# Attention and experts in one kernel: layer norm spread over two rounds a batch, routing one piece a round, tokens' transposes in other banks and ahead of the scores, idle matmuls at the start

## The chip, the cores and the metric

The kernel runs on one core of a Trainium2 chip. The core has a matrix engine (TensorE, PE in the profile), a vector engine (VectorE, DVE), a scalar engine (ScalarE, ACT), GpSimd (POOL) and SyncE (SP), which here only issues transfers. Each works through its own list of instructions in order and waits on semaphores for the others. The metric is the time of one execution on the device, in microseconds (us); less is better.

## The reference, cut to what matters

The input x has 8 batches of 512 tokens of 256 numbers, all in float32. Attention has 16 heads of 64, and the expert part has 16 experts with 1024 hidden units and 256 places each.

```python
xn  = layernorm(x)                                   # over the 256, eps 1e-5
# attention
q, k, v = split(xn @ qkv_w.T)                        # 16 heads of 64
q, k = rope(q), rope(k)
kb  = -max(p, .01) * log1p(max(a, .01) * |i - j|)    # a and p per head
attn = softmax(q @ k.T / 8 + kb)
att = concat(attn @ v) @ out_w.T
# experts
gate = softmax(xn @ Wg); idx = argmax(gate)          # one expert a token
loc  = place of the token among those of its expert  # kept if loc < 256
ffn  = relu(dispatched @ w1) @ w2, gathered back, times its gate
out = x + att + ffn
```

## The kernel before

**Steps and rounds.** The 16 heads are taken in 4 groups of 4. A step s is one group and one batch (32 steps, s = 8 g + b), and a step has four rounds (128 in all; d counts them, `dd` is d modulo 4). Each round projects one of q and k of a head pair for the next step (`project_qk`), computes the scores of the next round's two query chunks (`score`), and turns the exponentials of this round's two (`turn`, DVE transposes in blocks of 32). `project_v` makes the values in the first two rounds of a step. At the end of odd rounds `move` sends a pair's turned exponentials across partitions with 16 transfers of 128 KB and three small ones, all issued by SP. Four rounds later `attend` multiplies them with the values and `attended` scales the result on DVE; `project_out` adds a finished step's output to y, in the first round of a step two steps later.

**Order.** The order of the instructions on every engine is the order in which the program writes them (the schedule is manual). What the main loop (L819) says in round d therefore stands on each engine's list behind all that earlier rounds put there. Lists `later` and `stores` hold transfers until a later round; `stores` is emptied on POOL, one a round in rounds 0 and 1, and up to three a round after that.

**Layer norm.** In the first group each batch passes: load (`load_x`, L88), `moments` on DVE (L187: four pairs of statistics and aggregation), `deviations` (L193: three small operations on DVE, and a Newton iteration of 15 small ones on POOL, or of 10 on DVE), `normalise` on ACT (L231: four operations of 256 columns), `transpose_normed` (L246: eight PE transposes into two banks, and two copies of 512 columns), `logits` and `turn_logits` (L265, L278). The normalised tokens (to xrd) and their transposes (to xnd) are stored by POOL. The three later groups, and steps from 3 on in the first, read the transposes back (`load_normed`, on SP).

**Banks.** The accumulator's eight banks are four pools: `ps_sc` 4 (scores), `ps_mm` 2 (projections, values, output sums, expert hidden units), `ps_av` 1 (attention), `ps_po` 1 (logits, routing, expert output). A matmul into a bank waits until the bank's last reader is done.

**Start.** L785 to L815 are the work ahead of round 0: the rotation's tables, the bias tables of two head pairs (Ln on ACT), batch 0 and batch 1 normalised and transposed, q and k of both pairs of step 0. Round 0's loop body comes after two units of scores.

**Routing and experts.** `route` (L291) is a generator: each `yield` ends a piece. The loop takes two pieces a round from round 11 (L889), until all 18 are done. Two rounds after that, in round 22, `expert_in(0)` runs, and from round 23 `expert_work` (L522) gives units: four of hidden and four of output for each of 16 experts, 128 in all. A round takes 0, 1, 3 (4 in every fourth step) and 2 units, by its place in the step (L905). Weights of the next expert are loaded by SP into the same two buffers when the units that read them are done. The units must be over before round 108 (`late`), since results are gathered from there.

Of the kernel before, what the change touches and what calls it, by code (L numbers as in the profile page):

```python
# [9 lines left out]
F32 = mybir.dt.float32  # L10
I32 = mybir.dt.int32
BF16 = mybir.dt.bfloat16
AF = mybir.ActivationFunctionType
# [4 lines left out]
B, S, DM, H, D = 8, 512, 256, 16, 64  # L18
E, F = 16, 1024
P = 128  # L20
NTOK = B * S
NT = NTOK // P
TB = S // P
# [3 lines left out]
GC = HG * D  # L27
# [6 lines left out]
def attention_and_experts(  # L34
# [13 lines left out]
    nc = tc.nc  # L48
# [34 lines left out]
    wg = const.tile([P, 2, 32], F32, name="wg")  # L83

    first = zpool.tile([P, TB, TB, DM], F32, tag="z", name="xin_first")
    xin: dict = {b: first[:, b] for b in range(TB)}

    def load_x(b, eng):  # L88
        if b >= TB:
            xin[b] = early.tile([P, TB, DM], F32, tag="xin", name=f"xin_{b}", bufs=XB)  # L90
        eng.dma_start(xin[b], x[b].rearrange("(n p) d -> p n d", p=P))

    def load_group(g, eng):
        wq = wpool.tile([P, 2, 3 * GC], F32, tag="wq", name=f"wq_{g}")
# [6 lines left out]

    nc.scalar.dma_start(fr, freqs)
    nc.scalar.dma_start(ab[:, 0, :], bias_a.partition_broadcast(P))
    load_x(0, nc.sync)
    nc.gpsimd.dma_start(ab[:, 1, :], bias_p.partition_broadcast(P))
    weights = {0: load_group(0, nc.scalar)}
    nc.vector.memset(wg, 0.0)
# [12 lines left out]
    def bias_tables(g, pair, stage):  # L120

        for j in range(2):
            h = g * HG + 2 * pair + j
            if stage == 0:
                kb[h] = kbpool.tile([P, TB, KBW // P, 32], F32, tag="kb", name=f"kb_{h}")
                nc.scalar.activation(
                    kb[h], dist, AF.Ln, bias=1.0, scale=ab[:, 0, h : h + 1]
                )
            if stage == 1:
# [54 lines left out]
    rstd = const.tile([P, NT], F32, name="rstd")  # L184
    off = const.tile([P, NT], F32, name="off")

    def moments(b):  # L187
        for n in range(b * TB, (b + 1) * TB):
            st = early.tile([P, 6], F32, tag="st", name=f"bn_{n}", bufs=3)
            nc.vector.bn_stats(st, xin[b][:, n % TB, :])  # L190
            nc.vector.bn_aggr(mv[:, n, :], st)
# [51 lines left out]
        )  # L243
        xns[b] = xn

    def transpose_normed(b, pool=ps_mm, tag="mm", copy=nc.scalar.copy):  # L246
        xn = xns.pop(b)
        if b < 3:
            xnT = xpool.tile([P, 2, S], F32, tag="xnT", name=f"xnT_{b}")
            xnTs[b] = xnT  # L250
        else:
            xnT = early.tile([P, 2, S], F32, tag="xt", name=f"xnT_{b}", bufs=2)
        for mc in range(2):
            pt = pool.tile([P, S], F32, tag=tag, name=f"xt_{b}_{mc}")
            for i in range(TB):
                nc.tensor.transpose(
                    pt[:, i * P : (i + 1) * P], xn[:, i, mc * P : (mc + 1) * P], ident
                )
            copy(xnT[:, mc, :], pt)  # L259
        stores.append(lambda: nc.gpsimd.dma_start(xnd[b], xnT))  # L260
        xns[b] = xnT

    lgT: dict = {}

# [26 lines left out]
    def route():  # L291
# [131 lines left out]
        for part in range(4):  # L423
            for n in range(8 * part, 8 * part + 8):
                nc.vector.tensor_scalar(
                    rows[part][:, n % 8, :], slot, loc[:, n : n + 1], None, ALU.is_equal
                )
# [138 lines left out]
    def project_v(s, i2):  # L566
        g, b = divmod(s, B)
        wq, _ = weights[g]
        if i2 == 0:
            vals[s] = qkpool.tile([P, TB, GC], F32, tag="v", name=f"v_{s}")  # L570
        ps = ps_mm.tile([P, 2, GC], F32, tag="mm", name=f"v_{s}_{i2}")
        for i in range(2):
            c0 = (2 * i2 + i) * P
            for mc in range(2):
                nc.tensor.matmul(  # L575
                    ps[:, i, :], xnTs[s][:, mc, c0 : c0 + P], wq[:, mc, 2 * GC :],
                    start=(mc == 0), stop=(mc == 1),
                )
        nc.scalar.copy(vals[s][:, 2 * i2 : 2 * i2 + 2, :], ps)
# [198 lines left out]
    steps = NG * B  # L778
# [35 lines left out]
    k1 = project_qk(0, 1, 1, False)  # L814
    turn_by(nc.vector, k1[2], k1[0], k1[1], slice(0, S))  # L815

    routing = route()
    working = begin = None
    for d in range(duos):  # L819
# [39 lines left out]
        if d in (1, 3) or 5 <= d <= 10:  # L859
            turn_logits(d - 3 if d > 3 else d // 2)  # L860
        if dd in (0, 1):
            project_v(s, dd)
        (turn_last if final else turn)(*units[2 * d + 1])
        if dd == 1 and 3 <= s + 2 < steps:
            load_normed(s + 2)
        if half and not final:
            move(s, pair)
# [2 lines left out]
            later.append(lambda s=s: store_y(s - 2, s - 2 >= steps - B + 2))  # L870


        if d in (0, 2) or 4 <= d <= 9:
            logits(d - 2 if d > 2 else d // 2)
        if d in (2, 4, 6, 7):
            normalise(d)
        if d in (2, 4):
            normalise(d + 1)
        if d < 4:
            moments(d + 2)  # L880
        if d in (5, 6):
            moments(d + 1)
        if d == 1:
            deviations(2, 4, nc.gpsimd)
        if d == 3:
            deviations(4, 6, nc.gpsimd)
        if d in (5, 6):
            deviations(d + 1, d + 2, nc.gpsimd)
# [116 lines left out]
```

## Time and profile before

| what | value |
|---|---|
| median of 3 runs | 1298.36 us (1293.68 to 1299.41) |
| the profiled execution | 1296.84 us, span 1295.1 us |
| busy in the span: PE, DVE, ACT, POOL | 1222.4, 898.8, 612.3, 607.7 us |
| TensorE clock granted, mean | 0.98 |
| first scores start (L598) | 28.1 us |
| transfers | 264.66 MB, 204 GB/s |

The profile is one execution taken by the hardware profiler. A line of the busy-time view gives a stretch and the busy us of each engine in it. A line of the view of waits says which instruction waited for which, the us in total, how often, and the longest. In a timeline a line gives start, duration, engine, source line, operation, the tile written and the tiles read, sizes and how many; in square brackets stands the idle time before it and what ended it. PEld is PE's loading of weights, SPq an instruction that issues a transfer. A matmul in float32 is two instructions in the trace. The engines' shares are averages over parts with different limits, so the first 240 us have to be read by themselves.

### The profile page before, as it was taken

What the parts mean: (1) busy time and instruction counts of PE and PEld (TensorE: products, weight loads), DVE (VectorE), ACT (ScalarE), POOL (GpSimd) and SP (SyncE); (2) the same over time, 40 slices, a digit from 0 to 9 for tenths busy, and PEclk for the clock granted to TensorE, in tenths of its full rate; (3) what the DMA queues carried; (4) which work ended last, traced back from release to release, by engine and by line L of the source; (5) the groups of instructions that cost most, each with busy time, mean ns of one, the idle gap of its engine ahead of it and who ended that gap; (6) DMA issues with size and microseconds to landing.
All of it is one profiled execution on the core that took longest, in us unless ns stands there. A gap on an engine that the chain in (4) does not pass through costs nothing.

```text
span 1295.1 us, 17166 instructions
## 1 busy us (share of the span) xinstructions
PE 1222.4 (94%) x4986; PEld 664.9 (51%) x4986; DVE 898.8 (69%) x2270; ACT 612.3 (47%) x1425; POOL 607.7 (47%) x569
## 2 busy tenths in 40 slices
PE   4877999999999999999999999999999999999877
PEld 1334434455555555555555555556555555444434
DVE  6967899866556666566666666666666666888762
ACT  5565434544544434444464434344346443466551
POOL 3666434633543444444444434353344433578840
PEclk9988999999999999999999999999999999999988
DMA  4388778788867788878777688698788676889995
GB/s 131 84 245 275 190 176 214 209 209 213 224 190 194 206 216 216 246 181 229 202 192 224 171 222 215 180 242 213 198 214 234 169 208 156 223 223 229 237 234 141
DMA packets 184797, 264.66 MB, mean 204 GB/s; under 512 B 32176, under 2 KB 96448, under 8 KB 184704
## 3 DMA queue, kind: packets, MB, share of 16 engines
q1 hardware_dynamic: 177232, 241.51, 72.2%
q0 software_dynamic: 6368, 20.99, 5.6%
q10 hardware_dynamic: 1104, 1.07, 0.2%
q8 instruction: 40, 0.66, 0.2%
q14 instruction: 53, 0.43, 0.1%
HBM read 99.91 MB, written 31.44 MB: 101 GB/s over the span
## 4 chain that ended last, share of the span: by engine, by line
PE 73%; DMA 8%; DVE 7%; SPq 5%; ACT 4%; issue 2%; POOL 1%; ACTq 0%; DVEq 0%; POOLq 0%
PE sc L598 14%; PE av L691 14%; PE qk L549 14%; PE ph L494 8%; PE po L509 8%; PE v L575 7%; PE po L730 7%; SPq L636 4%; DMA pt<-z 4%; DVE z L609 2%; DVE z L622 1%; ACT z L613 1%; DMA w<-in_w 1%; SPq L644 1%; DMA early<-yd 1%
## 5 line engine op out<-in xcount | busy, mean ns | idle before, releaser
L562 POOL TENSOR_TENSOR t<-t,cos_t 128x512 f32<-128x512 f32 (+1 forms) x126 | 160.9, 1277 | 592.6 <-ACT t L558 587.2
L613 ACT ACTIVATE z<-z,st 128x512 f32<-128x512 f32 x512 | 363.3, 711 | 51.2 <-DVE st L609 34.8
L609 DVE CUSTOM_DVE_ANT_1 z<-sc,kb 128x512 f32<-128x512 f32 x512 | 322.7, 686 | 30.1 <-PE sc L598 24.8
L622 DVE STREAM_TRANSPOSE z<-z 128x512 f32<-128x512 f32 x504 | 320.1, 682 | 0.0
L598 PE MATMUL sc<-t,t 64*128 64x512 f32 x1024 | 258.3, 621 | 5.9 <-DVE t L564 3.6
L549 PE MATMUL qk<-xnT,wq 128*128 128x512 f32 x512 | 251.3, 615 | 6.9 <-ACT xnT L259 3.0
L558 ACT COPY t<-qk 128x512 f32<-128x512 f32 x125 | 73.0, 584 | 376.5 <-DVE sh L553 374.2
L691 PE MATMUL av<-pt,v 128*64 128x512 f32 x1008 | 233.8, 606 | 4.5 <-DMA rb<-rd 3.3
L598 PEld LDWEIGHTS sc<-t,t 64*128 64x128 f32 x1024 | 90.2, 188 | 165.5 <-issue 143.8
L553 DVE LOAD_MASK_SELECT sh<-qk x128 | 1.8, 14 | 244.5 <-PE qk L549 241.0
L564 POOL TENSOR_TENSOR t<-t,sh 128x512 f32<-128x512 f32 (+1 forms) x126 | 160.7, 1275 | 9.9
L563 POOL TENSOR_TENSOR sh<-sh,sin_t 128x512 f32<-128x512 f32 (+1 forms) x126 | 161.1, 1279 | 0.0
L691 PEld LDWEIGHTS av<-pt,v 128*64 128x64 f32 x1008 | 68.3, 138 | 161.6 <-issue 146.9
L549 PEld LDWEIGHTS qk<-xnT,wq 128*128 128x128 f32 x512 | 97.0, 196 | 91.7 <-issue 70.5
L575 PE MATMUL v<-wq,xnT 128*128 128x256 f32 x512 | 127.1, 392 | 8.2 <-ACT t L558 5.8
L730 PE MATMUL po<-wo,o 128*128 128x256 f32 x512 | 125.3, 388 | 2.9 <-ACT xnT L259 2.3
L494 PE MATMUL ph<-xdT,w 128*128 128x256 f32 x512 | 120.0, 385 | 4.6 <-ACT hT L500 1.9
L509 PE MATMUL po<-w,hT 128*128 128x256 f32 x512 | 120.8, 384 | 1.9 <-ACT hT L500 1.0
L575 PEld LDWEIGHTS v<-wq,xnT 128*128 128x128 f32 x512 | 95.8, 193 | 45.9 <-DVE z L622 21.1
L730 PEld LDWEIGHTS po<-wo,o 128*128 128x128 f32 x512 | 95.1, 191 | 39.4 <-ACT t L558 12.1
L494 PEld LDWEIGHTS ph<-xdT,w 128*128 128x128 f32 x512 | 95.2, 190 | 34.0 <-ACT t L558 6.8
L509 PEld LDWEIGHTS po<-w,hT 128*128 128x128 f32 x512 | 94.7, 190 | 31.1 <-issue 12.7
(145 smaller groups left out, 799.8 us busy)
## 6 DMA issues: line engine op xcount, KB each, us to landing
pt<-z SPq DMA_DIRECT2D x1008, 128.0 KB
w<-in_w SPq DMA_DIRECT2D x64, 512.0 KB
rb<-rd SPq DMA_DIRECT2D x126, 128.0 KB
xnT<-xnd SPq DMA_DIRECT2D x29, 512.0 KB
yd<-y SPq DMA_DIRECT2D x26, 512.0 KB
y<-yd SPq DMA_DIRECT2D x24, 512.0 KB
xrd<-xn POOLq DMA_DIRECT2D x8, 512.0 KB
xnd<-xnT POOLq DMA_DIRECT2D x8, 512.0 KB, 4.9
```

Of the source, the lines that this page charges most:

```text
L494: nc.tensor.matmul(ph[:, i, :], held["w1", e, fc // 4][:, mc, (fc % 4) * P : (fc % 4 + 1) * P], xdT[:, mc, :], start=(mc == 0), stop=(mc = ...
L509: nc.tensor.matmul(po[:, c, :], hT[:, fc, c * P : (c + 1) * P], held["w2", e, fc // 4][:, fc % 4, :], start=(fc == 0), stop=(fc == F // P ...
L549: nc.tensor.matmul(ps, wq[:, mc, c0 : c0 + P], xnTs[s][:, mc, :], start=(mc == 0), stop=(mc == 1),)
L562: eng.tensor_tensor(t[:, c], ps[:, c], cos_t[:, c], ALU.mult)
L563: eng.tensor_tensor(sh[:, c], sh[:, c], sin_t[:, c], ALU.mult)
L575: nc.tensor.matmul(ps[:, i, :], xnTs[s][:, mc, c0 : c0 + P], wq[:, mc, 2 * GC :], start=(mc == 0), stop=(mc == 1),)
L598: nc.tensor.matmul(sc[j].rearrange("p (g c k) -> p g c k", g=TB, k=32), q[r, qc * P : (qc + 1) * P], k[r, :].rearrange("p (c g k) -> p g c ...
L609: nc.vector.tensor_tensor_reduce(z, sc[j].rearrange("p (g c k) -> p g c k", g=TB, k=32), bias, -0.125, 3.0e38, ALU.add, ALU.min, st[:, j : ...
L613: nc.scalar.activation(z, z, AF.Exp, bias=st[:, j : j + 1], scale=-1.0, accum_out=sums[s, pair][:, j, qc : qc + 1],)
L622: nc.vector.transpose(z, z)
L691: nc.tensor.matmul(av[j * D : (j + 1) * D, :].rearrange("p (a q) -> p a q", q=P), vals[s][:, kc, c0 : c0 + D], pts[s, pair][:, j, :, kc, : ...
L730: nc.tensor.matmul(ps[:, i, :], oTs[pair][:, c0 : c0 + P], wot[:, pair, :], start=(pair == 0), stop=(pair == 1),)
```

## The change

The loads of x change place: batch 0 comes in two halves, batch 3 takes a buffer of y. Ahead of round 0, 42 idle matmuls of the identity (20, 8 and 14) are put into PE's list, batch 1's moments are split around batch 0's copies, its deviations go to POOL, the DVE turns 256 instead of 128 columns of q, and batch 1's transposes move behind the first scores. In the loop a batch's moments are taken in halves in two rounds (`moments_at`), it is normalised in a round of its own (`normal_at`) and transposed in the next but one or the next (`turned_at`), ahead of that round's scores. The transposes go to the banks of attention and of logits (for batch 2, of attention and projections) instead of the projections' two; the first half of the values goes to the attention's bank. Routing starts at round 16 with one piece a round, and the 32 compares yield every four instead of every eight. The experts take 1, 1, 4 and 2 or 3 units a round. The new stage 2 of `bias_tables` is called nowhere.

```diff
-    xin: dict = {b: first[:, b] for b in range(TB)}
-    def load_x(b, eng):
-        if b >= TB:
+    xin: dict = {b: first[:, b] for b in range(3)}
+    def load_x(b, eng, parts=1):
+        if b == 3:
+            xin[b] = ypool.tile([P, TB, DM], F32, tag="y", name=f"xin_{b}")
+        if b > 3:
...
-    load_x(0, nc.sync)
+    load_x(0, nc.sync, 2)
...
-    def moments(b):
-        for n in range(b * TB, (b + 1) * TB):
+    def moments(b, halves=(0, 1)):
+        for n in [b * TB + 2 * h + i for h in halves for i in range(2)]:
...
-    def transpose_normed(b, pool=ps_mm, tag="mm", copy=nc.scalar.copy):
+    def transpose_normed(b, copies=None):
         xn = xns.pop(b)
-        if b < 3:
+        if b < 4:
...
         for mc in range(2):
+            pool, tag = ((ps_av, "av"), (ps_mm, "mm") if b == 2 else (ps_po, "po"))[mc]
...
+    def keep_warm(n):
+        idle = ps_sc.tile([P, P], F32, tag="sc", name=f"idle_{len(idles)}")
+        idles.append(idle)
+        for _ in range(n):
+            nc.tensor.matmul(idle, ident, ident, start=True, stop=True)
...
+                if n % 4 == 3:
+                    yield
             if part > 1:
                 gathered(0, part - 2)
-            yield
...
-        ps = ps_mm.tile([P, 2, GC], F32, tag="mm", name=f"v_{s}_{i2}")
+        pool, tag = ((ps_av, "av"), (ps_mm, "mm"))[i2]
+        ps = pool.tile([P, 2, GC], F32, tag=tag, name=f"v_{s}_{i2}")
...
     bias_tables(0, 1, 0)
+    keep_warm(20)
     moments(0)
     deviations(0, 1, nc.vector)
     normalise(0)
+    keep_warm(8)
     rotation(1)
...
-    moments(1)
-    transpose_normed(0, ps_sc, "sc", nc.vector.tensor_copy)
-    deviations(1, 2, nc.vector)
+    moments(1, (0,))
+    transpose_normed(0, (nc.vector.tensor_copy, nc.vector.tensor_copy))
+    moments(1, (1,))
+    deviations(1, 2, nc.gpsimd)
     q0 = project_qk(0, 0, 0, False)
-    nc.scalar.copy(q0[2][:, P:], q0[0][:, P:])
-    turn_by(nc.vector, q0[2], q0[0], q0[1], slice(0, P))
     k0 = project_qk(0, 0, 1, False)
+    nc.scalar.copy(q0[2][:, 2 * P :], q0[0][:, 2 * P :])
+    normalise(1)
+    turn_by(nc.vector, q0[2], q0[0], q0[1], slice(0, 2 * P))
     turn_by(nc.vector, k0[2], k0[0], k0[1], slice(0, S))
-    turn_by(nc.gpsimd, q0[2], q0[2], q0[1], slice(P, S))
-    normalise(1)
-    transpose_normed(1, ps_sc, "sc")
+    keep_warm(14)
     score(*units[0])
     score(*units[1])
+    turn_by(nc.gpsimd, q0[2], q0[2], q0[1], slice(2 * P, S))
     bias_tables(0, 1, 1)
     project_qk(0, 1, 0)
+    transpose_normed(1)
     k1 = project_qk(0, 1, 1, False)
...
+    moments_at = {0: [(2, 0), (2, 1)], 2: [(3, 0)], 3: [(3, 1)], 4: [(4, 0)], 5: [(4, 1)],
+                  6: [(5, 0)], 7: [(5, 1)], 9: [(6, 0)], 10: [(6, 1)], 11: [(7, 0)], 12: [(7, 1)]}
+    normal_at = {1: 2, 5: 3, 7: 4, 9: 5, 11: 6, 13: 7}
+    turned_at = {3: 2, 6: 3, 8: 4, 10: 5, 12: 6, 14: 7}
...
+        if d in turned_at:
+            transpose_normed(turned_at[d])
         if d + 1 < duos:
             score(*units[2 * d + 2])
...
-        if 3 <= d <= 8:
-            transpose_normed(d - 1)
...
-        if d == 5:
-            load_x(6, nc.gpsimd)
-            load_x(7, nc.gpsimd)
+        if d in (8, 10):
+            load_x(d // 2 + 2, nc.gpsimd)
...
+        if d in normal_at:
+            normalise(normal_at[d])
+        for b1, h in moments_at.get(d, ()):
+            moments(b1, (h,))
+            if h == 1:
+                deviations(b1, b1 + 1, nc.gpsimd)
+        if d >= 16 and routing:
+            for _ in range(1):
-        if d >= 11 and routing:
-            for _ in range(2):
...
-            for _ in range((0, 1, 3 + (s % 4 == 0), 2)[dd]):
+            for _ in range((1, 1, 4, 2 + s % 2)[dd]):
```

The loop before took the moments of batch d + 2 whole in rounds 0 to 3 and of batch d + 1 in rounds 5 and 6, the deviations of batches 2 and 3, and 4 and 5, together, and normalised those pairs together in rounds 2 and 4 (batches 6 and 7 in rounds 6 and 7). In the changed kernel logits follow in the round of the transposes, their turn in the round after.

More of the change, by code (lines that the diff above doesn't have):

```diff
@@ L85, in attention_and_experts @@
     first = zpool.tile([P, TB, TB, DM], F32, tag="z", name="xin_first")
-    xin: dict = {b: first[:, b] for b in range(TB)}
-    def load_x(b, eng):
-        if b >= TB:
-            xin[b] = early.tile([P, TB, DM], F32, tag="xin", name=f"xin_{b}", bufs=XB)
-        eng.dma_start(xin[b], x[b].rearrange("(n p) d -> p n d", p=P))
+    xin: dict = {b: first[:, b] for b in range(3)}
[3 more added lines that the diff above has]
+        if b > 3:
+            xin[b] = early.tile([P, TB, DM], F32, tag="xin", name=f"xin_{b}", bufs=XB)
+        w = TB // parts
+        for i in range(parts):
+            eng.dma_start(
+                xin[b][:, i * w : (i + 1) * w],
+                x[b, i * w * P : (i + 1) * w * P].rearrange("(n p) d -> p n d", p=P),
+            )
     def load_group(g, eng):
@@ L128, in bias_tables @@
                 )
+            if stage == 2:
+                nc.scalar.activation(kb[h], kb[h], AF.Copy, scale=ab[:, 1, h : h + 1])
+                nc.scalar.activation(kb[h], kb[h], AF.Copy, scale=-8.0)
             if stage == 1:
@@ L258, in transpose_normed @@
                 )
-            copy(xnT[:, mc, :], pt)
+            (copies or (nc.scalar.copy,) * 2)[mc](xnT[:, mc, :], pt)
         stores.append(lambda: nc.gpsimd.dma_start(xnd[b], xnT))
         xns[b] = xnT
+    def keep_warm(n):
[3 more added lines that the diff above has]
+            nc.tensor.matmul(idle, ident, ident, start=True, stop=True)
+    idles: list = []
     lgT: dict = {}
@@ L858, in attention_and_experts @@
             attended(*was)
-        if d in (1, 3) or 5 <= d <= 10:
-            turn_logits(d - 3 if d > 3 else d // 2)
+        if d == 1:
+            turn_logits(0)
+        if d == 3:
+            turn_logits(1)
+        if d - 1 in turned_at:
+            turn_logits(turned_at[d - 1])
         if dd in (0, 1):
@@ L863, in attention_and_experts @@
         (turn_last if final else turn)(*units[2 * d + 1])
-        if dd == 1 and 3 <= s + 2 < steps:
+        if dd == 1 and 4 <= s + 2 < steps:
             load_normed(s + 2)
@@ L870, in attention_and_experts @@
             later.append(lambda s=s: store_y(s - 2, s - 2 >= steps - B + 2))
[L873 to L888, printed above, removed]
-        if d >= 11 and routing:
-            for _ in range(2):
+        if d in (0, 2):
+            logits(d // 2)
+        if d in turned_at:
+            logits(turned_at[d])
+        if d in normal_at:
[6 more added lines that the diff above has]
+            for _ in range(1):
                 if routing and next(routing, True):
```

## The prediction

> **What bounds the kernel now.** I read first the slices of the page and busy time by stretches of 50 us (columns: stretch, us, busy PE, PE weight load, DVE, ACT, POOL with instruction counts, TensorE clock, DMA share, GB/s).
>
> ```profile
> 0.00:50.00 50.00, 30.09 (x98) 13.76 (x99) 37.42 (x111) 25.93 (x45) 19.45 (x28) 0.93 0.30 96
> 50.00:100.00 50.00, 36.84 (x170) 16.63 (x170) 38.91 (x120) 30.06 (x73) 33.87 (x61) 0.90 0.80 226
> 100.00:150.00 50.00, 44.59 (x227) 20.89 (x229) 36.32 (x101) 28.24 (x69) 28.45 (x47) 0.93 0.81 229
> 150.00:200.00 50.00, 44.24 (x156) 22.52 (x153) 46.51 (x115) 21.69 (x55) 24.16 (x26) 0.93 0.77 184
> 200.00:250.00 50.00, 48.87 (x230) 22.44 (x230) 46.19 (x134) 21.32 (x54) 22.77 (x19) 0.97 0.77 199
> 500.00:550.00 50.00, 49.16 (x205) 28.82 (x202) 31.74 (x78) 20.72 (x51) 21.94 (x19) 1.00 0.87 239
> ```
>
> From about 240 us on TensorE is the bound and nearly gapless; the first 240 us are where it waits, and the change works there. Next, who makes PE wait in 0 to 240 us:
>
> ```profile
> PE xt L256 <- ACT xn L235: 15.1, 8, 13.5
> PE v L575 <- ACT t L558: 5.8, 2, 3.2
> PE xt L256 <- ACT t L558: 4.7, 2, 2.5
> PE sc L598 <- DVE t L564: 3.6, 1, 3.6
> PE qk L549 <- ACT xnT L259: 3.0, 1, 3.0
> PE lgp L271 <- DVE lg L281: 2.7, 2, 2.4
> PE v L575 <- ACT xnT L259: 2.3, 1, 2.3
> PE po L730 <- ACT xnT L259: 2.3, 1, 2.3
> PE sc L598 <- POOL rstd L214: 2.3, 1, 2.3
> ```
>
> (The 13.5 is the start, before anything can run.) Normalising, transposing (xt, xnT) and its two "mm" banks stand in most rows. One case from the timelines of ACT and PE, in round 3:
>
> ```profile
> 61.40 4.04 ACT L235 ACTIVATE xn<-xin_first,off,rstd 128x256 f32<-128x256 f32 x8
> 69.72 1.07 ACT L259 COPY xnT<-xt 128x512 f32<-128x512 f32 x2 [0.58 <-DMA xnd<-xnT]
> 70.36 3.78 PE L549 MATMUL qk<-xnT,wq 128*128 128x512 f32 x4 [2.97 <-ACT xnT L259]
> ```
>
> Two batches are normalised at once on ACT, the copy waits for a store of the tile it overwrites, PE waits 2.97 us and then runs at half clock (3.78 for what takes 1.92 later). Last, a step (4 rounds) late in the run, without experts, from 1125.70 to 1155.10: the same PE work, undisturbed.
>
> ```profile
> 1125.70:1155.10 29.40, 29.40 (x114) 13.66 (x112) 25.48 (x65) 16.82 (x43) 21.39 (x18) 1.00 0.87 215
> ```
>
> So 29.4 us is PE's floor for a step without experts, its rounds (score start to score start, from the PE timeline) 9.0, 9.1, 3.8, 7.4; DVE needs 25.5 of it. An expert unit costs 1.73 (a round of 10.87 against 9.14). Before, round 0's scores start at 38.1, round 9's at 118.0, round 16's at 186.9.
>
> **What the Trainium skill says.** The Trainium skill, "TensorE: Matmul & The Clock Gate", section "Part 1: The HAM clock gate (the 'warmup' mystery)": an idle PE is at half clock until some 3.4 us of sustained work. Agrees: projections step by 0.85 us until 20 us and by 0.43 after, and the clock is 0.84 and 0.81 in 20 to 40 us. The same page and part, under "Architectural detail": ACT and DVE queues are strict FIFO. Agrees: the ACT copy above holds all behind it. The Trainium skill, "GPSIMD Engine Reference", section "1. Specifications": its SBUF interface is shared with VectorE where DVE has two SBUF inputs. Agrees: DVE's 128x512 multiply took 1.45 beside POOL, 0.67 with one input in PSUM. The Trainium skill, "DMA: Bandwidth & Descriptors", section "Issuing engines are not separate DMA queues": transfers of all queues share the same 16 engines. So moved loads on POOL still compete; share is 0.93 to 1.0 in 55 to 80 us.
>
> **The change, part by part.**
>
> Start. DVE loses 10 small operations of 0.16 to 0.2 (deviations of batch 1 go to POOL, some 4.2 us there by the row of batch 2-3: 57.06 to 61.33) and half of batch 1's moments (4 instructions, 1.05 us) move behind the xnT copies. 42 warm-up matmuls are 84 instructions (a projection's two are four in the trace); by the transposes' 0.14 each warm, twice that cold, the first 56 run from 4.5 (identity ready) to 14 or 15 us. The transposes' last input comes at 14.8, so they cost 0 to 1 us; unhidden the 84 would be 12 to 23. Walk: xnT ready 16.5 (was 17.5), q projected 18.3, k 20.0 (warm), two shuffles to 20.8, q's first half and k turned on DVE (about 5.5 beside POOL) to 26.3, scores 26.4 (was 28.1) at 1.92 instead of 3.78. Then q of pair 1, batch 1's transposes, k of pair 1 at 32.2; its turn 3.6 on DVE; round 0's first DVE score operation at 37.5 (was 41.5). Gain 4.0.
>
> Rounds 0 to 8 are DVE's. A round there is a shuffle 0.62, four score operations and four transposes at 0.61 (5.5), 0.35 more in odd rounds, 0.6 for a normalised head pair in odd rounds from 5, 1.2 for two output sums where due; a half batch of moments is 1.05, the three-instruction head of the deviations 0.6. Before, rounds 0 to 3 carry four batches' moments; now batches 2 and 3, and later halves are spread. After, by round 0 to 8: 8.2, 6.0, 6.6, 7.6, 6.7, 8.2, 6.6, 8.3, 6.9, sum 65.1: round 9 at 102.6. PE's own sums (1.92 each for scores, projection, values, an output sum; attention 3.6; transposes 1.09; logits 0.65 and 0.27: 6.4, 6.0, 5.6, 4.8, 6.0, 10.4, 4.5, 8.8, 9.7) stay under this. Add 2 in round 3: batch 2's tile is still being stored. POOL issues that store after round 2's turn, near 57; it lands 5 later at 62 to 63, the copies end at 64, the next projection's shuffle starts at 67 instead of 65. Round 9: 104.6, against 119.2 for the same operation before.
>
> Rounds 9 to 15 are PE's: 10.5, 4.5, 8.8, 9.7, 10.5, 4.5, 7.7 (floor, with transposes 1.09 and logits 0.65 + 0.27), sum 56.2. The transposes now stand ahead of the scores, so a late xn holds the scores, and behind them values and projections: in round 12 normalise ends (after the exponentials) some 2.4 later than PE arrives, elsewhere 1. Batch 6's load is issued on POOL in round 8 behind deviations and a turn, near 103, and lands near 109 (5.2 before); DVE wants it at 108: 1 to 2. Together 5. Two waits on SP are new: the y load of round 6 needs batch 3's tile normalised (round 5, earlier), and xnT 4's load of round 9 needs its store, issued on POOL near 104 and landed near 110; behind it stands round 9's move, ready at 109: at most 1, within the 5. Round 16's scores: 104 + 56 + 5 = 165, was 186.9. Gain so far 22, of which 4 is the start. The other banks (av, po) take away the waits of v and po on "mm"; their own readers (one DVE operation after the attention, 4 us before the next use) are early enough.
>
> Rounds 16 to 38, routing. 22 pieces, one a round. Its DVE work is some 25 us in all (32 compares: 16 take 4.27):
>
> ```profile
> 209.45 4.27 DVE L425 TENSOR_SCALAR rows<-slot,loc 128x256 bf16<-128x256 f32 x16
> ```
>
> 1.15 a round, so DVE needs 25.5 + 4.6 = 30.1 a step, PE 29.4 + 1 for routing's matmuls, and SP:
>
> ```profile
> 174.18 2.58 SPq L636 DMA_DIRECT2D pt<-z  x4
> 176.86 0.93 SPq L641 DMA_DIRECT2D rd<-turned  x1
> 177.83 8.65 SPq L636 DMA_DIRECT2D pt<-z  x12
> 186.53 1.28 SPq L644 DMA_DIRECT2D rb<-rd  x2
> ```
>
> 13.6 a pair, 27 a step, with three more issues 29. Three queues at 29 to 30: I take 31.2 a step. Over 5.75 steps 1.8 x 5.75 = 10.4 above the floor, and 2 for the tables of the next head group in rounds 29 to 32. Before, rounds 16 to 22 were 12.8 above the floor and round 30 stood 3.3 (PE on ACT). Gain 3.7; bounds: -14 (34.3 a step, as rounds 12 to 15 now) to +16 (no loss).
>
> Experts. They begin at round 41 instead of 23; 128 units at 8 or 9 a step, which ends at 101 (was 105). PE's sum is the same; steps of 43 to 45 us hide everything else. In six places weights are reloaded within four units and one pair of rounds, 14.3 us (before in two, with no visible wait); the waits above 0.8 us before sum to 5.5. I take 0, bounds -8 and +4. The end of the kernel is unchanged: 0.
>
> Sum: 22 + 3.7 + 0 = 25.7. From the profiled execution, 1296.8 (span 1295.1), 1271.1. That execution is 1.5 under the median of the runs, 1298.4, so I forecast 1272.5.
>
> **The rivals.** (a) The wait moves: rounds without experts reach 41 instead of 23, and DVE, SP and DMA (share 0.77 to 0.87 where a step took 29 to 34) hold a step at 34.3. Then rounds 16 to 40 lose 14 instead of winning 4 (3.1 x 5.75 = 18 apart): 25.7 - 18 = 8, about 1290. For it: nothing in the trace shows 29.4 with routing; against: the late steps hold 29.4 at a share of 0.87 with gathers besides. (b) The six short reloads wait 2 each: 1284. (c) The change does not do what it says: DVE's total work to round 16 is unchanged but for 2 us, and if DVE, not its order, set the pace, only the start's 4 us remain: 1294. Against: DVE has 25 of 100 us free in 50 to 150. (d) Slower: SP's move of a pair. It took 22.6 to 23.3 us from one to the next in rounds 3 to 9, with DMA saturated. If that holds for rounds 8 to 40, a step is 46 at worst; above 34.4 a step over these 8 steps the gain (25.7) is gone; at 37, 46 lost, about 1319. Against: there SP also waited for late work.
>
> **How the numbers follow.** Forecast 0.70, own range 1262 to 1282; (a) 0.14; (b) 0.06; (c) 0.05; (d) 0.05. A measurement here tells 0.5% (6.5 us) from nothing. Faster: 0.70, 0.06 and most of (a), 0.12: 0.88. Same: the rest of (a) and (c), 0.07. Slower 0.05. Without the 5 of rounds 3 to 15 and the 12 of routing it would end at 1255; the low end goes two thirds of that way: 1260. The high end reaches into (a): 1287.
>
> **What would show it.** Right: round 0's score operations near 37 to 38, warm scores at 26; round 9 near 104, round 16 near 165; rounds 16 to 40 at 31 us a step, no waits of v or po on copies of xnT; experts gapless. Wrong: PE waiting on xn ahead of the scores for over 3 us in a round, routing steps over 33, PE on weights in rounds 55 to 63 or 87 to 95.

## The result, and the profile after

| kernel | median, us | runs, us | ratio to before |
| --- | --- | --- | --- |
| before | 1296.0 | 1289.2 to 1299.4 | 1 |
| changed | 1274.9 | 1271.8 to 1280.1 | 0.9841, 95% interval 0.9817 to 0.9865 |

The changed kernel is 1.6% faster: 21 us, where 25.7 were forecast. Its profiled execution (1280.1, span 1278.4) is the slowest of its four runs, so the two profiles differ by 16.7 us only. I read it in the order of the prediction. Busy time by stretches (columns as before) of the changed kernel:

```profile
0.00:50.00 50.00, 42.45 (x219) 26.30 (x220) 40.48 (x122) 32.26 (x61) 29.69 (x61) 1.00 0.33 100
50.00:100.00 50.00, 42.23 (x188) 19.35 (x186) 44.90 (x134) 30.17 (x76) 35.98 (x70) 0.93 0.86 223
100.00:150.00 50.00, 48.21 (x232) 23.28 (x230) 41.01 (x113) 29.18 (x72) 34.38 (x57) 1.00 0.96 264
150.00:200.00 50.00, 45.33 (x179) 19.98 (x180) 43.15 (x107) 24.59 (x62) 26.57 (x28) 0.94 0.90 227
200.00:250.00 50.00, 49.78 (x193) 24.06 (x190) 44.85 (x114) 23.69 (x60) 23.25 (x19) 1.00 0.83 200
```

PE gains 12 us of busy time in the first stretch (mostly the warm-up: without it the stretch has 31.7 us instead of 42.5), 5 in the second, 4 in the third, and only 1 in the fourth, where the DMA share was 0.77 and is now 0.90. What PE waits for, up to round 41 (0 to 365 us):

```profile
PE lgp L291 <- ACT xnT L270: 6.9, 1, 6.9
PE qk L570 <- DMA xnT<-xnd: 5.9, 3, 3.7
...
PE xt L267 <- ACT xn L245: 1.8, 11, 0.2
PE qk L570 <- ACT t L579: 1.6, 1, 1.6
```

The five rows of before in which transposes, values, projections and output sums wait for ScalarE's copies out of an accumulator (v and xt on t, qk, v and po on xnT: 5.8 + 4.7 + 3.0 + 2.3 + 2.3 = 18.1 us) are gone but for 0.2 us; the 1.6 of projections that wait for the copy of q or k stood at 1.4 before. Transposes wait for xn 1.8 us in all, not over 0.2 at a time. Two larger waits are left: logits in round 3, and a new row, projections that wait for a load of a transposed batch. Scores by round, from PE's timeline (start of the scores, and for the operation on them the first one of VectorE):

| | before | changed | gain |
| --- | --- | --- | --- |
| first scores | 28.1 | 22.7 | 5.4 |
| round 0's score operation | 41.5 | 34.2 | 7.3 |
| round 9's scores | 131.3 | 104.5 | 26.9 |
| round 16's scores | 186.9 | 162.8 | 24.1 |
| round 20's scores | 227.4 | 198.6 | 28.8 |
| round 108's scores | 1113.9 | 1089.9 | 24.0 |
| end of span | 1295.1 | 1278.4 | 16.7 |

Everything is won by round 16; rounds 16 to 108 take 927.0 and 927.1 us; the rounds from 108 on lose 7 us in this pair of profiles.

The place of the new wait is round 19. PE's timeline there, then SyncE's (issue times; x12 is a group of twelve):

```profile
194.90 3.75 PE L570 MATMUL qk<-xnT,wq 128*128 128x512 f32 x4 [3.70 <-DMA xnT<-xnd]
```

```profile
172.03 13.05 SPq L658 DMA_DIRECT2D pt<-z  x12
185.13 1.29 SPq L666 DMA_DIRECT2D rb<-rd  x2
186.52 0.55 SPq L742 DMA_DIRECT2D yd<-y  x1
187.18 0.37 SPq L235 DMA_DIRECT2D xnT<-xnd  x1
```

The load of the transposed batch for step 6 stands behind a move whose twelve issues take 13.05 us, and lands when PE has waited 3.70; then step 6's first projection takes 3.75 us, where the one at 182.84 us took 1.98. Round 19 takes 13.8 us from scores to scores. That is rival (a), in one place.

### The profile page after: what moved, and what is told of

Read it like the earlier page. It is cut to its first block, busy times and chain, and to the rows that moved or that the text cites. A ratio compares the mean times of both kernels' runs of the same rounds, so it can differ in the third digit from the quotient of the medians.

```text
span 1278.4 us, 17383 instructions
## 1 busy us (share of the span) xinstructions
PE 1219.7 (95%) x5070; PEld 670.1 (52%) x5070; DVE 893.5 (70%) x2265; ACT 611.7 (48%) x1425; POOL 617.4 (48%) x614
## 4 chain that ended last, share of the span: by engine, by line
PE 71%; DMA 13%; DVE 6%; SPq 5%; ACT 3%; issue 1%; POOL 1%; ACTq 0%; DVEq 0%
PE sc L620 13%; PE qk L570 13%; PE av L713 12%; PE po L752 8%; PE v L597 8%; PE ph L515 8%; PE po L530 7%; DMA xnT<-xnd 5%; SPq L658 4%; DMA pt<-z 4%; DMA w<-in_w 3%; DVE z L631 2%; DVE z L644 1%; ACT z L635 1%; ACT xn L245 1%
## 5 line engine op out<-in xcount | busy, mean ns | idle before, releaser
L570 PE MATMUL qk<-xnT,wq 128*128 128x512 f32 x512 | 247.8, 607 | 12.6 <-DMA xnT<-xnd 8.1
L620 PE MATMUL sc<-t,t 64*128 64x512 f32 x1024 | 255.3, 617 | 0.7 <-DVE t L585 0.7
L570 PEld LDWEIGHTS qk<-xnT,wq 128*128 128x128 f32 x512 | 94.4, 192 | 101.5 <-issue 69.0
L597 PE MATMUL v<-wq,xnT 128*128 128x256 f32 x512 | 124.1, 385 | 0.0
L597 PEld LDWEIGHTS v<-wq,xnT 128*128 128x128 f32 x512 | 94.7, 190 | 35.8 <-DVE z L644 14.6
```

Source lines behind the costliest of these rows:

```text
L570: nc.tensor.matmul(ps, wq[:, mc, c0 : c0 + P], xnTs[s][:, mc, :], start=(mc == 0), stop=(mc == 1),)
L597: nc.tensor.matmul(ps[:, i, :], xnTs[s][:, mc, c0 : c0 + P], wq[:, mc, 2 * GC :], start=(mc == 0), stop=(mc == 1),)
L620: nc.tensor.matmul(sc[j].rearrange("p (g c k) -> p g c k", g=TB, k=32), q[r, qc * P : (qc + 1) * P], k[r, :].rearrange("p (c g k) -> p g c ...
```

## The experiments

All ratios are to the kernel before. Kernels whose ends lie less than some 6 us apart have overlapping intervals; for these the rounds of the traces have to decide, of one execution each, which repeat to about 0.2 us up to round 19's scores (changed kernel, two profiles: round 16 at 162.8 and 162.9).

| run | median, us | ratio | 95% interval | round 16 | round 20 | round 41 | round 108 to end |
| --- | --- | --- | --- | --- | --- | --- | --- |
| changed, again | 1273.4 | 0.9835 | 0.9812 to 0.9857 | 162.9 | 198.3 | 363.0 | 183.3 |
| old accumulators | 1293.1 | 0.9981 | 0.9968 to 0.9995 | 180.2 | 209.6 | 380.8 | 188.6 |
| old accumulators and place | 1293.0 | 0.9994 | 0.9977 to 1.0011 | 182.9 | 212.3 | 383.9 | 183.8 |
| old place | 1279.0 | 0.9868 | 0.9835 to 0.9902 | 175.5 | 204.9 | 366.9 | 186.5 |
| two batches at once | 1279.3 | 0.9875 | 0.9843 to 0.9907 | 168.4 | 200.4 | 367.8 | 187.9 |
| no warm-up | 1277.1 | 0.9877 | 0.9844 to 0.9910 | 165.3 | 201.2 | 366.8 | 183.6 |
| earlier store | 1276.6 | 0.9863 | 0.9840 to 0.9886 | 162.2 | 199.3 | 366.3 | 185.0 |
| two pieces a round | 1282.5 | 0.9921 | 0.9897 to 0.9946 | 162.4 | 196.4 | 416.6 | 187.6 |
| loads on GpSimd | 1263.3 | 0.9763 | 0.9740 to 0.9785 | 163.0 | 193.8 | 355.5 | 180.6 |
| loads, store, logits | 1262.2 | 0.9747 | 0.9723 to 0.9772 | 161.2 | 198.9 | 360.9 | 180.3 |
| before, pace alone | 1290.6 | 0.9976 | 0.9960 to 0.9992 | 182.3 | 213.2 | 382.9 | 185.1 |
| before, loads on GpSimd | 1292.7 | 1.0001 | 0.9982 to 1.0019 | 187.1 | 227.6 | 437.4 | 180.4 |

(Round 41 of kernels whose experts begin earlier is not comparable: before, its variant with the loads, and two pieces.)

**The changed kernel again**, unaltered.

> The changed kernel once more, as the measure for the three runs beside it. My theory: 0.984 of the time before again, and the last stretch (from round 108's scores to the end), which took 188.5 us in the profile shown against 181.3 before, varies from execution to execution, so that a second profile has it at 181 to 186. Rival: the 188.5 belongs to the change and stands again within 1.5 us.

The last stretch took 183.3 us, so 5 of the 7 us lost there were that execution's. Over the whole, 22 us are won.

**The transposes' and values' accumulators as before.**

```diff
-            pool, tag = ((ps_av, "av"), (ps_mm, "mm") if b == 2 else (ps_po, "po"))[mc]
+            pool, tag = ps_mm, "mm"
...
-        pool, tag = ((ps_av, "av"), (ps_mm, "mm"))[i2]
+        pool, tag = ps_mm, "mm"
```

> The changed kernel with the transposes and the values in the two accumulators that projections also use, as before. Theory: the waits of values and projections for copies on ScalarE return (in the profile of before 15 us of such waits stood in rounds 0 to 22, part of them beside VectorE's own work): round 16's scores 3 to 8 us later, the end 2 to 8 later than the changed kernel. Rival: VectorE sets rounds 0 to 8 and the waits lie in its shadow: round 16 within 1 us and the end within 1.5.

0.9981: nearly the whole gain is gone, more than either theory had. Round 16's scores come at 180.2, 17.3 us late. (Before, batches 0 and 1 were transposed into the scores' accumulators; here they too go into the projections' two. Round 0's score operation comes 1.5 us later by it, so up to 1.5 of the 17.3 are not the old state's.) PE's waits from 30 to 365 us:

```profile
PE xt L267 <- ACT t L579: 12.6, 6, 5.6
PE v L597 <- ACT t L579: 6.7, 5, 2.0
```

A transpose now follows a projection directly and needs both of the projections' accumulators; one of them is full until ScalarE's copy of q or k (line 579). ScalarE is seldom what makes that copy late. The longest wait, in PE's timeline and ScalarE's:

```profile
57.21 1.11 PE L267 MATMUL xt<-ident,xn 128*128 128x128 f32 x4 [5.63 <-ACT t L579]
```

```profile
56.57 0.58 ACT L579 COPY t<-qk 128x512 f32<-128x512 f32 x1 [2.87 <-DVE sh L574]
```

ScalarE had been idle for 2.87 us: the copy waits for VectorE's shuffle of the same projection, which the program puts ahead of it and which VectorE reaches only after score operations, four transposes and half a batch's moments. So the accumulator is emptied in the order of VectorE's list too. The copies ahead of the waits at 102.8 and 144.1 us had waited 2.8 and 2.1 us for the shuffle, those in the routing steps up to 4.2; the copy at 28.2 us came straight behind exponentials, and that at 84.8 after normalising and 0.7 us of waiting.

The second row is the values' wait in the routing steps, all five after 210 us, 0.5 to 2.0 us each (round 24 takes 11.2 instead of 9.5). Up to round 16 PE waits at transposes and not at values; in rounds 20 to 41, where no batch is transposed, the kernel takes 171.2 us instead of 164.7. By this the loss up to round 16 is the transposes', and some 6.5 us after round 20 are the values'. Between them, in rounds 16 to 20, 6 us come back (29.4 us instead of 35.4), with no wait for a load in this profile.

**Place and accumulators as before.**

```diff
-        if d in turned_at:
-            transpose_normed(turned_at[d])
         if d + 1 < duos:
...
             attend(*was)
+        if d in turned_at:
+            transpose_normed(turned_at[d])
```

and the two lines of the experiment above.

> The changed kernel with both the place and the accumulators of the transposes as before (behind scores and attention, in the projections' two accumulators, and the values with them). Theory: place and accumulators hang together: ahead of the scores a transpose comes directly behind a projection, finds its accumulators still full and holds everything (12 to 14 us of such waits); behind them they have been emptied. So the old accumulators cost little here: round 16's scores at 175 to 181, the end at 1279 to 1285. Rival: the accumulators cost their 20 us wherever the transposes stand: round 16 at 192 or later, the end at 1295 or more.

The rival for the end (0.9994), though round 16 comes at 182.9, near my theory's 181. My idea that accumulators matter only ahead of the scores falls: the waits change their names, not much their size (26.4 us in these four rows, 24.8 in the four largest of the kernel above). PE's waits, 30 to 365 us:

```profile
PE lgp L291 <- ACT xnT L270: 9.8, 4, 2.7
PE v L597 <- ACT t L579: 6.7, 5, 2.0
PE po L752 <- ACT xnT L270: 5.5, 2, 2.7
PE xt L267 <- ACT t L579: 4.4, 3, 3.0
```

**The place alone as before**, with the new accumulators (the diff just shown, without the accumulators' lines).

> The changed kernel with the transposes behind the scores and the attention of their round, as before, everything else of the change kept. Theory: the scores no longer wait for a late batch, but the transposes' copies and logits, and the next projection, come 2 to 5 us later in the six rounds concerned; as the batch is ready when the round begins (waits of 0.2 us), little hangs on it: round 16's scores 0 to 3 us later, the end 0 to 3 later. Rival: the place ahead of the scores is what carries the gain: round 16 6 us or more later, and so the end.

Neither. Round 16 is 12.6 us late, as the rival had it, but the end only 5.6. PE's largest wait, 30 to 365 us:

```profile
PE lgp L291 <- ACT xnT L270: 15.1, 4, 6.4
```

Behind scores and attention, the copies come late in ScalarE's order and the round's logits wait for them, with the next projection behind. Rounds 16 to 20 then take TensorE's floor, 29.4 us, against 35.4, and rounds 20 to 41 162.0 against 164.7: more than half of the delay is made up. No projection waits for a load in this profile (there is no such row from 30 to 365 us), where the changed kernel had 5.9 us of it.

**Two batches at once.**

```diff
-    moments_at = {0: [(2, 0), (2, 1)], 2: [(3, 0)], 3: [(3, 1)], 4: [(4, 0)], 5: [(4, 1)],
-                  6: [(5, 0)], 7: [(5, 1)], 9: [(6, 0)], 10: [(6, 1)], 11: [(7, 0)], 12: [(7, 1)]}
-    normal_at = {1: 2, 5: 3, 7: 4, 9: 5, 11: 6, 13: 7}
+    moments_at = {0: [(2, 0), (2, 1)], 1: [(3, 0), (3, 1)], 4: [(4, 0), (4, 1)],
+                  5: [(5, 0), (5, 1)], 8: [(6, 0), (6, 1)], 9: [(7, 0), (7, 1)]}
+    normal_at = {2: (2, 3), 6: (4, 5), 10: (6, 7)}
...
-        if d in (8, 10):
-            load_x(d // 2 + 2, nc.gpsimd)
+        if d == 7:
+            load_x(6, nc.gpsimd)
+            load_x(7, nc.gpsimd)
...
-            normalise(normal_at[d])
+            for b1 in normal_at[d]:
+                normalise(b1)
```

> The changed kernel with whole batches' moments in one round and two batches normalised at once on ScalarE, as before; the transposes stay in the rounds and the place that the change gave them. Theory: this is the part that the gain from round 1 to round 16 (17 us beyond the start) comes from: rounds 1, 5, 6, 8 and 10 lengthen, since 4 us of ScalarE work stand ahead of the exponentials and copies, and round 16's scores start 5 to 10 us after 162.8, the end 4 to 10 later than the changed kernel. Rival: where the transposes stand and their banks matter, not the spreading: round 16 within 2 us, the end within 2.

The theory: round 16 5.5 us late, the end 5.9. The largest wait of PE is a new one ahead of round 3's scores, for batch 2, which is normalised a round later and as one of two (the edit does both, and they were not taken apart):

```profile
PE xt L267 <- ACT xn L245: 6.2, 1, 6.2
```

So the spreading is a part of the gain, but neither the only one nor the largest. By round 20 all but 2.1 us had been made up; the loss comes back later, in routing steps and at the end, so its size at the end is less certain than that at round 16.

**No warm-up.**

```diff
-    keep_warm(20)
...
-    keep_warm(8)
...
-    keep_warm(14)
```

> The changed kernel without the 42 matmuls that keep TensorE at work at first; nothing else differs. Theory: first transposes, projections and scores run at half clock, the first scores start some 3 us later and take 3.8 us instead of 2.0, round 0's first score operation on VectorE comes 4 to 6 us later than 34.2, and since VectorE sets rounds 0 to 8 the delay stays to the end: 4 to 6 us more than the changed kernel. Rival: the backlog of SyncE and the DMA engines in rounds 8 to 20 swallows it: round 20's scores start within 1 us of 198.6, and the time is the same within 1.5 us.

The first scores come at 24.7 instead of 22.7, round 0's score operation at 37.1 instead of 34.2: 2.9 us, under the 4 to 6 expected. At round 20 2.9 are still there (201.2), at round 108 1.7. The theory in kind, at some half to two thirds of its size in the rounds. At the end the profiled executions are 1.9 us apart, the medians 3.7 and the ratios 5.4, with intervals that overlap.

**The store of batch 0's transposes a round earlier.**

```diff
-        if d == 0:
-            stores[1:3] = reversed(stores[1:3])
```

> The changed kernel with batch 0's transposes stored one round earlier, so that the copy of batch 2's transposes in round 3 finds its buffer free. Theory A: round 3 falls from 13.8 us to 7 or 8, and the gain of 6 us stays: 5 to 7 us less than the changed kernel. Theory B: the gain is there at round 4, but from round 8 to 20 SyncE's queue and the DMA engines set the pace (34.6 us a step), which start no sooner, so that round 20's scores are at most 2 us earlier, and so is the end.

Neither theory. ScalarE's copy no longer waits, yet round 3 still takes 13.0 us (13.9 in the changed kernel), since another wait stood 0.7 us under the first. PE's timeline and then VectorE's in round 3:

```profile
59.01 1.08 PE L291 MATMUL lgp<-xnT,wg 128*32 128x128 f32 x16 [6.24 <-DVE lg L301]
```

```profile
58.68 0.18 DVE L301 COPY lg<-lg 128x64 f32<-128x64 f32 x1
```

The logits of batch 2 need the one "po" accumulator, and VectorE empties it of batch 1's turned logits only after four score operations and two transposes of the round. And even the 0.7 is lost at round 19 (15.1 us, 4.6 of them waiting for the load).

**The loads of transposed batches on GpSimd.**

```diff
-        nc.sync.dma_start(xnT, xnd[s % B])
+        nc.gpsimd.dma_start(xnT, xnd[s % B])
```

> The changed kernel with the loads of transposed batches issued by GpSimd instead of SyncE, so that they no longer stand behind a move of twelve transfers. Theory: round 19 loses the 3.7 us wait of the projection for its load and takes 10 instead of 13.8, smaller ones in other steps go too: 2 to 5 us less than the changed kernel. Rival: the DMA engines' share (0.92 to 0.96) is what delays the load, not its place in the queue: the wait comes back elsewhere, and the time is the same within 1.5 us. A third: GpSimd issues later than SyncE, because its turns stand ahead, and TensorE waits more: 2 to 6 us more.

The theory, at twice its size: 1263.3, 10 us less than the changed kernel and 2.4% less than before; faster than both. Up to round 19 nothing moves (184.9 and 185.0); then, in PE's timeline and GpSimd's:

```profile
191.91 1.98 PE L570 MATMUL qk<-xnT,wq 128*128 128x512 f32 x4
```

```profile
179.84 0.60 POOL L235 DMA_DIRECT2D xnT<-xnd  x1 [2.15 <-PE v L597]
```

The load is issued 7.3 us earlier and the projection runs warm without a wait. Round 20 comes 4.5 us earlier; rounds 20 to 41 give 3.0 more, rounds 41 to 108 3.0, the last stretch 2.7, each against the second profile of the changed kernel. In that profile PE waits for such loads four times, 7.5 us in all (3.1 of it in round 19), so these waits can be most of the gain (10 us by the medians, 13 between the two profiles), but not all; where the rest comes from was not followed. The DMA engines are as full as before (share 0.94 in 180 to 200 us, 0.90 in the second profile of the changed kernel), so the place in the queue was the cause in round 19, not their load.

**The same edit in the kernel before.**

> The kernel before with the loads of transposed batches issued by GpSimd instead of SyncE, as in the changed kernel's variant that won 10 us. Theory: before the change no projection waited for such a load, since everything came later, and so there was no wait to take away: within 3 us of before. Rival: the queue's order is worth 8 to 12 us in this kernel whatever the order of the rounds, and the same is seen here.

1.0001: the theory, though its reason holds only up to the last stretch, where the kernel before has one such wait, of 1.4 us. The queue's order cost next to nothing while everything came later; the change made it a cost.

**Loads, store and logits together.** The edits of the two kernels above, and

```diff
+        if d == 3:
+            turn_logits(1)
         (turn_last if final else turn)(*units[2 * d])
...
-        if d == 3:
-            turn_logits(1)
```

> The changed kernel with the loads on GpSimd, batch 0's transposes stored a round earlier, and batch 1's logits turned ahead of round 3's first head pair instead of after it. Theory: round 3's slip has two layers, the store and, 0.7 us beneath it, the logits' accumulator that VectorE empties only after six operations of the round; with both gone the time from round 3's first score operation to round 4's falls from 10.4 us to 7.6 to 8.2, and since the loads no longer wait behind the moves this reaches the end: 2 to 3 us less than with the loads on GpSimd alone, 1260 to 1261. Rival: SyncE and the DMA engines set the pace of rounds 8 to 20 all the same: round 20's scores within 0.7 us of 193.8 and the same time within 1 us as with the loads alone (1263.3).

The rival in time, 1262.2, the same as with the loads alone, but not in round 20, which comes 5.1 us later than there. Round 3 is 2.0 us shorter (12.0), less than expected, since VectorE's copy still comes behind the four score operations. Round 19 in this profile loses it and more, PE's timeline, then SyncE's:

```profile
190.88 6.20 PE L713 MATMUL av<-pt,v 128*64 128x512 f32 x16 [5.67 <-DMA pt<-z]
```

```profile
173.47 15.25 SPq L658 DMA_DIRECT2D pt<-z  x12
```

With the load out of the way, it is the move itself that is late: its twelve issues took 15.25 us, against 12.31 for the same move (from 170.46 us) in the kernel with the loads alone, where the attention waits 1.32. Since the median is no worse, this 5.67 need not be in every execution.

**The pace alone, in the kernel before.**

```diff
-        if d >= 11 and routing:
-            for _ in range(2):
+        if d >= 16 and routing:
+            for _ in range(1):
...
-            for _ in range((0, 1, 3 + (s % 4 == 0), 2)[dd]):
+            for _ in range((1, 1, 4, 2 + s % 2)[dd]):
```

and routing's compares in fours.

> The kernel before with the routing from round 16 on, one piece a round, its compares in fours, and the changed kernel's pace of experts; nothing else of the change. Theory: TensorE's sum is the same, and routing and experts have little idle time to give back: 0 to 4 us less than before. Rival: the pace is where the gain of 21 us comes from: 8 us less or more. Third: what the late experts leave in rounds 23 to 40 is bound by VectorE and the moves, and 2 to 6 us are lost.

The theory: 0.9976, some 3 us. But round 16 comes at 182.3, 4.6 us earlier than before, because no routing stands in rounds 11 to 15 any more. In the changed kernel, too, rounds 11 to 15 are free of routing; so some 4.6 of the 24.1 us that it has won by round 16 are, by this estimate, work put off.

**Two pieces of routing a round, in the changed kernel.**

```diff
-            for _ in range(1):
+            for _ in range(2):
```

and the compares in eights.

> The changed kernel with two pieces of routing a round (compares in eights, so 18 pieces), so that routing ends some 12 rounds earlier, experts begin near round 27, and end earlier by as much. Theory: routing's VectorE work then takes over 2 us a round and VectorE comes after TensorE in rounds 16 to 26, but the rounds without experts between are fewer: the two cancel, 0 to 4 us more than the changed kernel. Rival: one piece a round is what the gain rests on: 6 us more or worse. The other side: rounds without experts are what loses (17 us above TensorE's sum from 16 to 41), and it is 3 us faster or better.

9 us more than the changed kernel (11 by the ratios), so the rival for the time. Its reason doesn't hold: rounds 16 to 20, with two pieces each, take 33.9 us, less than the 35.4 of one piece. The losses lie where routing ends and experts begin: round 24 takes 17.1 us and round 31 17.7, the first with PE waiting on ScalarE's copy and the second, in PE's timeline, on an expert's weights:

```profile
311.50 2.90 PE L514 MATMUL ph<-xdT,w 128*128 128x256 f32 x8 [2.71 <-DMA w<-in_w]
```

Of the 9, the profiled execution shows 2.6 at round 108 and 4.3 in the last stretch, beside the second profile of the changed kernel; why routing's pace should reach to the last rounds was not settled.

## Why the prediction was right, and where not

**The start: right in kind, too small (4.0; 7.3 measured).** The term that was mis-sized is the turn of q's first half and k on VectorE, taken as 5.5 us beside GpSimd. It took 3.1 (19.55 to 22.67 us); the two shuffles ahead of it were done 1.2 us sooner than forecast. The multiply concerned, in VectorE's timelines of before and after:

```profile
25.14 1.43 DVE L563 TENSOR_TENSOR sh<-sh,sin_t 128x512 f32<-128x512 f32 x1
```

```profile
21.27 0.68 DVE L584 TENSOR_TENSOR sh<-sh,sin_t 128x512 f32<-128x512 f32 x1
```

GpSimd was at work in both, in the first on 128x896 elements, in the second on deviations of 128x4. The warm-up matmuls were hidden, as said, and carry 2.9 of the 7.3, which the prediction had counted only as the warm rate of scores and projections.

**Rounds 0 to 8: the order of VectorE's work is right in six rounds of nine.** Forecast 8.2, 6.0, 6.6, 9.6 (with the 2 for the store), 6.7, 8.2, 6.6, 8.3, 6.9; measured between first score operations 8.2, 5.9, 6.5, 10.4, 6.9, 9.6, 6.5, 8.3, 9.0. Rounds 5 and 8 are off by 1.4 and 2.1: I used VectorE's sum in each, where TensorE's (10.4 and 9.7 in the same paragraph; 10.8 and 9.8 from scores to scores) was the larger; that TensorE's sums "stay under this" was a misreading of my own figures. Round 3's slip has a second layer, which the prediction did not see: the store alone was worth 0.7 to 0.9 us. Start and rounds err against each other: round 9 was forecast for 104.6 and came at 105.6. The figure set beside it from before is wrong by a round: 118.0 and 119.2 are round 8's; round 9's are 131.3 and 132.5. Round 16's, which the sum uses, is right.

**Rounds 9 to 15: right.** 56.2 + 5 forecast, 58.4 measured. Of the 5 for late batches, loads and the store hardly half appeared: transposes waited 0.2 at a time. (Before, the same rounds took 55.6 with routing and without transposes.)

**What carries it: not priced.** The prediction gave the accumulators a single sentence without a number. It took its gain from the order of VectorE's work and from TensorE's floor, and its sums for rounds 0 to 15 took every wait on an accumulator as gone. The runs say that this assumption carries the gain. Four kernels differ only in the place of the transposes and in the two accumulator lines; the end as a ratio to before, then round 16's scores:

| | transposes behind the scores | ahead of them |
| --- | --- | --- |
| old accumulators | 0.9994, 182.9 | 0.9981, 180.2 |
| new accumulators | 0.9868, 175.5 | 0.9835, 162.9 |

With neither, all the rest of the change (start, warm-up, spreading, pace) brings nothing that shows: round 16 at 182.9, where the new pace alone has 182.3. The new accumulators are worth 16 to 19 us of the end, in either place. The new place is worth 4 to 6 with them and some 2 without, both within overlapping intervals. By round 16 it is the pair that counts: 7.4 us for the accumulators alone, 2.7 for the place alone, 20.0 for both. The spreading (5.5 at round 16, some 6 at the end) and the warm-up (2 to 5) were taken out only beside the new accumulators. So the parts don't add up. The new accumulators alone, in the kernel before, were not run; whether they need the rest is open.

Could the price have been read from the waits before? The five rows on copies sum to 18.1 us, near to what the old accumulators lose, but the nearness is in part luck. 3.0 of it is round 4's first projection (70.36 us), which also needs the very tokens that are being copied; 3.2 lies after round 16's scores; 11.9 are left, part of them in rounds that VectorE sets. Rival (c)'s figure, 1294, is near the kernels with the old accumulators (1293.1 and 1293.0), but not for its reason, since not even the start's 4 us are left there.

The Trainium skill, "Perfetto Trace Analysis", section "Matmuls" (under "Optimizing Tensor Performance"), says that independent groups of matmuls should rotate through different PSUM banks, so that emptying one overlaps the next group; this case agrees, and gives the price of two banks for five users: 1.3 to 1.5%.

**Routing, rounds 16 to 40: the rate right, one step wrong.** 31.2 a step forecast; rounds 20 to 40 took 31.1. But rounds 16 to 20 took 35.8 (35.4 in the second profile), over the 33 that the prediction had named as a sign of being wrong, by the load behind the move: rival (a)'s mechanism, for one step instead of six. The prediction had looked at that load's queue ("behind it stands round 9's move") and asked what waits behind the load, not what the load waits behind. Over rounds 16 to 108 3.7 were to be won, and 0 were (1.6 in the second profile). Rival (d), a move that holds every step at 37, was not seen, but its cause, a move's issues taking up to 15 us, is what one profile of the kernel with loads, store and logits met next.

**Experts: right.** Between 365 and 1090 us PE waited 3.3 us for weights in all; rival (b) is out.

**The end: 0 forecast, 7 lost in the pair of profiles, 2 in the second profile.** With the loads on GpSimd it takes 180.3 to 180.6 (before 181.3), and in ten profiles of kernels with the new pace and the loads on SyncE 183.3 to 188.6. So a loss of 2 to 7 belongs to those loads at the new pace. In the profile shown PE waits there 8.3 us for a move to land (4.1 before, 4.7 in the second profile) and 2.2 for loads (1.4 and 3.4); how the two hang together was not followed up.

Sum: 24.1 by round 16 (22 forecast), 0 to round 108 (3.7), some 2 lost at the end (0): 22, where 25.7 was forecast. Ratio and range held by errors of both signs, so in part by luck, and on an assumption that had not been examined.

## What to carry to other kernels

Add up the waits by what must be emptied before they end, not only by the waiting line: rows of three operations were mostly one cause, two accumulators, and a reordering brought next to nothing at the end until these were split. Then follow the emptying one step further back: the copy that frees an accumulator may itself wait for another engine's list, here VectorE's shuffle. When work upstream becomes earlier, look along each in-order queue for what an urgent transfer stands behind; here a one-word edit, worthless before, gave nearly half as much again as the change. And test a change of several parts by taking parts out: the parts' losses (accumulators 20, place 6, spreading 6, warm-up 4, by the medians) add up to more than the gain of 22.

## What was not expected of the hardware

VectorE's 128x512 multiply with both inputs in SBUF took 1.43 us beside GpSimd's 128x896 scaling of a table, and 0.68 beside GpSimd operations of 128x4, one every 0.3 us. And where GpSimd's 128x256 multiply began while VectorE was at its 128x512 addition (22.0 us in the changed kernel), VectorE took its usual 0.69 and GpSimd 1.26, against 0.72 for its next one; in this one place it was the later of the two that took longer.

SyncE's issue of twelve transfers of a move took 12.31 and 7.64 us for two moves in a row of one kernel (from 170.5 and 189.2 us, loads on GpSimd) and 15.25 in another (from 173.5 us, loads, store and logits), with the DMA share between 0.84 and 0.94 around it.
